# A fused four-layer kernel: first batch's steps and weight splits reordered, a smaller weight ring, more raw buffers, and extra products on TensorE

## The chip, the core and the metric

The kernel runs on one core of a Trainium2 chip. The metric is the time of one execution on the device in microseconds (us). TensorE is named PE in the profile, its weight loads PEld, VectorE is DVE, ScalarE is ACT, GpSimd is POOL, and SP is the engine that issues most of the transfers.

## The reference

The input x has 16 batches of 256 positions and 256 channels. Four layers follow each other, each added to x. Cut to what matters:

```python
# layer 0, for each batch: gates, 16 decaying scans over the positions, a small gated network, a normalisation
ctx = causal_ema(x, tau_ctx)
gated = x * sigmoid(concat(x, ctx) @ Wg.T + bg)
mod = 0.5 + sigmoid(gelu(x @ Wn1.T + bn1) @ Wn2.T + bn2)           # 16 factors for each position
traces = causal_ema(gated * mod[d], tau_raws[d])                    # d = 0..15
temporal = sum_d traces[d] * softmax(blend)[d]
x += layernorm((gelu(x @ Wsoma.T + bsoma) * sigmoid(temporal @ Wtemp.T + btemp)) @ Wout.T)
# layer 1: masked softmax pooling over the 256 positions
s = tanh(x @ W1 + b1) @ v
x += softmax(where(mask, s, NEG)) @ x / cnt
# layer 2: 8 experts and a shared one, all dense
x += sum_e coef[b, e] * ((silu(x @ Wg[e]) * (x @ Wu[e])) @ Wd[e])
# layer 3: 256 -> 1024 -> 256, a part of its second matrix chosen for each batch
x += gelu(x @ W1 + b1) @ concat(W2, We[indices[b]]) + bias
```

Layers 2 and 3 hold nearly all of the products.

## The kernel before

**Precision.** For most products each operand is split into a rounded part and a remainder (`rnd` on one engine, then `low` on another), and `mm3` (L101 to L104) makes three products of them. The first batch's layers 0 and 1 do without the split: `first_traces` and `first_pooled` make plain fp32 products.

**Layers 0 and 1** are written as generators, one per batch: `traces` (21 steps) and `pooled` (10 steps), with `first_traces` (13 steps) and `first_pooled` for batch 0. `feed` interleaves the steps of two neighbouring batches: batch 0's pooling runs beside the first steps of batch 1's traces. In `first_traces`, ph and pg are the first products, hg is a Gelu of ph, pm a product of hg, md its Tanh; from these come the 16 factors, then 16 scans of two halves each on VectorE, which TensorE adds up in PSUM (ta0). In `first_pooled` the names follow each other in a chain: t, pt, g, po, rs (a power on POOL), x1, four transposes ptr, x1T, pa, th, psc, sc (softmax), four transposes ppt, q, pp, acc, and the split x2 that the experts read. `evict(c, ...)` (L470 to L476) copies PSUM to SBUF on ScalarE for c = 0 and on VectorE for c = 1.

**Layers 2 and 3** follow a written plan of units. A chunk of an expert is 128 x 768 values (`w_e`). Batch 0 is alone for the first five experts, two chunks to a unit; batch 1 joins at the sixth ("boards"), and afterwards pairs of batches share each chunk. Each `l2_unit` makes products pg and pu, ScalarE and VectorE make h of them, ScalarE and POOL split it (hh), and the downward products (y) are issued two units later (LAG). At the end of a pair's experts come eight chunks of layer 3 (`w_f`, products q and z), with chunks chosen by batch (`w_c`).

**Weights.** `load_chunk` fetches a chunk into one of two raw buffers, rounds it on ScalarE (`w_e<-raw_e`, L89) and takes the remainder on VectorE or POOL (L96) into one of RING = 10 tiles. A chunk that has been split twice before is stored in DRAM and later reloaded whole (`w_e<-keep_e`). `prefetch` runs through the chunks in the plan's order. The small weights of layers 0 and 1 are split once (`split_small`), some before the scans' end and some beside batch 1's traces.

**Order.** The tile framework arranges the instructions of each engine by a simulated timeline, under priorities. `tc.issue_after(i)` keeps what stands under it from being arranged ahead of instruction i. `last_of` remembers such instructions. Each engine then works through its own queue in order.

Of the kernel before, what the change touches and what calls it, by code (L numbers as in the profile page):

```python
# [8 lines left out]
F32 = mybir.dt.float32  # L9
F32R = mybir.dt.float32r  # L10
I32 = mybir.dt.int32
AF = mybir.ActivationFunctionType
ALU = mybir.AluOpType
# [4 lines left out]
S = 256  # L18
# [1 line left out]
ND = 16  # L20
NE = 8
NF = 8
RING = 10
FRONT = 4
FRONT0 = 3
SLACK = 16
# [19 lines left out]
def fused_kernel(  # L46
# [24 lines left out]
    xin = ctx.enter_context(tc.tile_pool(name="xin", bufs=2))  # L71
    l0 = ctx.enter_context(tc.tile_pool(name="l0", bufs=1))
    ring = ctx.enter_context(tc.tile_pool(name="ring", bufs=RING))
    raws = ctx.enter_context(tc.tile_pool(name="raws", bufs=2))
    xs = ctx.enter_context(tc.tile_pool(name="xs", bufs=3))
    accp = ctx.enter_context(tc.tile_pool(name="accp", bufs=3))
    hp = ctx.enter_context(tc.tile_pool(name="hp", bufs=2))
# [59 lines left out]
    def split_small(c0, n, e):  # L137
        rnd("a", wh[:, c0 : c0 + n], small(c0, n))
        low(e, wl[:, c0 : c0 + n], small(c0, n), wh[:, c0 : c0 + n])
# [114 lines left out]
    def ft(tag, name, bufs=1):  # L254
        return l0.tile([P, 2, S], F32, tag=tag, name=name, bufs=bufs)
# [5 lines left out]
    def traces(b):  # L261

        xr = xin_tiles.pop(b)
        xh, xl = hl(f"x_{b}", "hA")
        rnd("a", xh, xr)
        low("g", xl, xr, xh)
        cx = ft("ta", f"ctx{b}")
        for c in range(2):
            V.tensor_tensor_scan(
                cx[:, c], decay[:, ND : ND + 1].to_broadcast([P, S]), xr[:, c], 0.0, ALU.mult, ALU.add  # L270
            )
        yield
        ch, cl = hl(f"c_{b}", "hA")
        rnd("a", ch, cx)
        low("v", cl, cx, ch)

        ph = ps_l.tile([P, 512], F32, tag="ps", name=f"ph{b}")
        for k in range(2):
            o = O_N1 + k * P
            mm3(ph[:, :S], W(0, o, P), W(1, o, P), xh[:, k], xl[:, k], k == 0, k == 1)  # L280
        hg = l0.tile([P, S], F32, tag="hg", name=f"hg{b}")
        A.activation(hg, ph[:, :S], AF.Gelu, bias=vec[:, V_BN1 : V_BN1 + 1])
        hs = l0.tile([P, S], F32R, tag="hs", name=f"hs{b}")
        rnd("a", hs, hg)
        low("v", hs[64:], hg[64:], hs[64:])
        yield
        pm = ps_l.tile([P, 512], F32, tag="ps", name=f"pm{b}")
        PE.matmul(pm[:48, :S], n2[:, 0], hs, start=True, stop=False)
        PE.matmul(pm[:48, :S], n2[:, 1], hs, start=False, stop=True)
        md = l0.tile([48, S], F32, tag="md", name=f"md{b}")  # L290
        A.activation(md, pm[:48, :S], AF.Tanh, bias=hb[:48, V_BN2 : V_BN2 + 1], scale=0.5)
        V.tensor_scalar(md, md, 0.5, 1.0, ALU.mult, ALU.add)
        mdd = dram.tile([1, ND, S], F32, tag="mdd", name=f"mdd{b}")
        nc.sync.dma_start(mdd[0], md[0:ND])
        yield
        pg = ps_l.tile([P, 2, S], F32, tag="ps", name=f"pg{b}")

        ga = ps_a.tile([P, 2, S], F32, tag="ga", name=f"gp{b}")
        for m in range(2):
            for k in range(4):  # L300
                o = O_G + k * S + m * P
                xa, xb_ = (xh[:, k], xl[:, k]) if k < 2 else (ch[:, k - 2], cl[:, k - 2])
                mm3(pg[:, m], W(0, o, P), W(1, o, P), xa, xb_, k == 0, k == 3)
        for m in range(2):
            A.activation(ga[:, m], pg[:, m], AF.Tanh, bias=hb[:, V_BG + m : V_BG + m + 1], scale=0.5)
        V.scalar_tensor_tensor(ga, ga, 1.0, xr, ALU.add, ALU.mult)
        yield
        sm = ft("sm", f"sm{b}")

        def soma():  # L310
            pso = ps_l.tile([P, 2, S], F32, tag="ps", name=f"pso{b}")
            for m in range(2):
                for k in range(2):
                    o = O_SO + k * S + m * P
                    mm3(pso[:, m], W(0, o, P), W(1, o, P), xh[:, k], xl[:, k], k == 0, k == 1)
            for m in range(2):
                A.activation(sm[:, m], pso[:, m], AF.Gelu, bias=vec[:, V_BSO + m : V_BSO + m + 1])

        tacc = ft("ta", f"ta{b}")
        for d in range(ND):  # L320
            if d % 2 == 0:
                mod = l0.tile([P, 2, S], F32, tag="mod", name=f"mod{b}_{d}", bufs=2)
                nc.sync.dma_start(mod, mdd[0, d : d + 2].partition_broadcast(P))
            bt = ft("bt", f"bt{b}_{d}", 3)
            tr = tacc if d == 0 else ft("tr", f"tr{b}_{d}", 3)
            with tc.issue_after(last_of[0].ins) if b == 1 and "h" not in last_of else nullcontext():
                for c in range(2):
                    V.scalar_tensor_tensor(
                        bt[:, c], ga[:, c], bl[:, c, d : d + 1], mod[:, d % 2], ALU.mult, ALU.mult
                    )  # L330
            for c in range(2):
                V.tensor_tensor_scan(  # L332
                    tr[:, c], decay[:, d : d + 1].to_broadcast([P, S]), bt[:, c], 0.0, ALU.mult, ALU.add
                )
            if d:
                G.tensor_tensor(tacc, tacc, tr, ALU.add)  # L336
            if b == 1 and d in rest:
                split_small(*rest[d], "g")
            if d == 5:
                soma()  # L340
            yield
        th, tl = hl(f"t_{b}", "hA")
        rnd("a", th, tacc)
        low("v", tl, tacc, th)
        xt = xt_tiles.pop(b)
        G.tensor_tensor(xt, xt, bet.unsqueeze(1).to_broadcast([P, 2, S]), ALU.add)
        held[b] = xt, sm, th, tl
        yield
# [122 lines left out]
    def evict(c, o, i):  # L471
# [3 lines left out]
        else:  # L475
            last_of["cv"] = V.tensor_copy(o, i)  # L476

    def first_traces():
        xr = xin_tiles.pop(0)
        cx = ft("ta", "ctx0")  # L480
        for c in range(2):
            last_of["cx"] = V.tensor_tensor_scan(
# [77 lines left out]
    def first_pooled():  # L560
# [19 lines left out]
        rs = l0.tile([P, 2], F32, tag="rs", name="rs0")  # L580
        for k in range(2):
            for t in range(2):
                PE.matmul(po[t], sg[:, k, t * P : (t + 1) * P], small(O_OU + k * S, S), start=k == 0, stop=k == 1)
        x1 = ft("x1", "x10")
        for t in range(2):
            V.bn_stats(st[:, t], po[t])
            V.bn_aggr(mv[:, t], st[:, t])
        V.tensor_scalar(rs, mv[:, :, 1], 4e-5, None, ALU.add)
        G.tensor_tensor(rs, rs, mhalf, ALU.pow)
        for t in range(2):  # L590
            V.scalar_tensor_tensor(po[t], po[t], mv[:, t, 0:1], gam, ALU.subtract, ALU.mult)
        yield
# [6 lines left out]
        ptr = two("ptr0")  # L599
        for c in range(2):  # L600
            for t in range(2):
                PE.transpose(ptr[c][:, t * P : (t + 1) * P], x1[:, t, c * P : (c + 1) * P], ident)
        x1T = ft("xo", "x1T0")
        for c in range(2):
            evict(c, x1T[:, c], ptr[c])
        yield
        pa = ps_l.tile([P, 512], F32, tag="ps", name="pa0")
        for k in range(2):
            PE.matmul(pa[:, :S], small(O_W1 + k * P, P), x1T[:, k], start=k == 0, stop=k == 1)
        ta = l0.tile([P, S], F32, tag="th", name="th0")  # L610
        last_of["ca"] = A.activation(ta, pa[:, :S], AF.Tanh, bias=vec[:, V_B1 : V_B1 + 1])
        yield
        psc = ps_l.tile([P, 512], F32, tag="ps", name="psc0")
        PE.matmul(psc[:, :S], vec[0:64, V_V : V_V + 1].to_broadcast([64, P]), ta[0:64], start=True, stop=True)

        sc = ft("sc", "sc0")
        mx = l0.tile([P, 2], F32, tag="mx", name="mx0")
# [9 lines left out]
        for j in range(2):  # L627
            js = slice(j, j + 1)
            V.tensor_tensor(sums[:, js], sums[:, js], cntb[:, 0, js], ALU.mult)
            V.reciprocal(sums[:, js], sums[:, js])  # L630
            last_of["cv"] = V.tensor_scalar(sc[:, j], sc[:, j], sums[:, js], None, ALU.mult)
        yield
        ppt = two("ppt0")
        for l in range(2):
            for j in range(2):
                PE.transpose(ppt[l][:, j * P : (j + 1) * P], sc[:, j, l * P : (l + 1) * P], ident)
        q = ft("bt", "q0", 3)
        for l in range(2):
            evict(l, q[:, l], ppt[l])
        yield  # L640
        pp = two("pp0")
        for l in range(2):
# [17 lines left out]
    def load_chunk(key):  # L660
# [26 lines left out]
        e = "v"  # L687
        if kind == "e" and key[1] == 0:

            e = "g" if key[2] < 2 else "v" if key[2] < 6 else "gv"[key[2] % 2]  # L690
        elif kind == "e" and key[1] < ALONE and key[2] % 3 == 0:
            e = "g"
        low(e, t[:, 1, :n], raw[:, :n], t[:, 0, :n])
# [251 lines left out]
            with tc.issue_after(last_of["cx"].ins):  # L945
                later_constants()
    with tc.issue_after(last_of["a"].ins), tc.issue_after(last_of["g"].ins), tc.issue_after(last_of["tr"].ins):
        for off, n in ((O_N1, 256), (O_G, 512), (O_G + 512, 512)):
            split_small(off, n, "g")
        prefetch(2, 0)  # L950


    n = 2
    while n_done[0] < 1:
        with tc.issue_after(last_of["ca"].ins), tc.issue_after(last_of["cv"].ins):
            next(steps)
            if n_steps[0] > FIRST + 5 and n < 6 and n_steps[0] % 2:
                prefetch(1, 0)
                n += 1
    with tc.issue_after(last_of["ca"].ins), tc.issue_after(last_of["cv"].ins):  # L960
        coefs()
        prefetch(RING - n)
# [155 lines left out]
```

## Time and profile before

| | us |
|---|---|
| median of 3 runs | 2840.18 (2839.82 to 2841.34) |
| the profiled execution, its own time | 2841.92 |
| span of that execution | 2840.2 |
| granted TensorE clock, mean | 0.994 |
| first product of an expert | 58.90 |
| TensorE busy | 2779.2 (98%) |
| VectorE, ScalarE, POOL busy | 1425.2, 1235.4, 1299.0 |

The span runs from the first to the last recorded instruction. Times inside it are counted from its start. Rows of the timeline read: start, duration, engine, source line, operation, what is written from what is read, sizes, count, and in brackets the idle time before it with what ended it. A wait row reads: who, for whom, us in total, times, longest. In a window row the pairs are the busy times of PE, PEld, DVE, ACT and POOL, each with its count of instructions, then the granted clock of TensorE, the share of the DMA engines and GB/s.

### The profile page before, as it was taken

What the parts mean: (1) busy time and instruction counts of PE and PEld (TensorE: products, weight loads), DVE (VectorE), ACT (ScalarE), POOL (GpSimd) and SP (SyncE); (2) the same over time, 40 slices, a digit from 0 to 9 for tenths busy, and PEclk for the clock granted to TensorE, in tenths of its full rate; (3) what the DMA queues carried; (4) which work ended last, traced back from release to release, by engine and by line L of the source; (5) the groups of instructions that cost most, each with busy time, mean ns of one, the idle gap of its engine ahead of it and who ended that gap; (6) DMA issues with size and microseconds to landing.
All of it is one profiled execution on the core that took longest, in us unless ns stands there. A gap on an engine that the chain in (4) does not pass through costs nothing. (4 is left out here: it accounts for less than half of the span.)

```text
span 2840.2 us, 36878 instructions
## 1 busy us (share of the span) xinstructions
PE 2779.2 (98%) x13604; PEld 2335.0 (82%) x13604; DVE 1425.2 (50%) x2646; ACT 1235.4 (43%) x2043; POOL 1299.0 (46%) x986
## 2 busy tenths in 40 slices
PE   7889989999999999999999999999999999999998
PEld 4877779888888888888888888888888888888887
DVE  7888766665665364544545445453444542222222
ACT  5555544546444533435334443334433453323433
POOL 5764654544544353544534445444444443333333
PEclk9999999999999999999999999999999999999999
DMA  4444645546443533324433153331523242222552
GB/s 125 136 148 122 196 162 181 185 131 230 148 164 117 180 115 104 119 77 135 150 110 106 40 180 112 111 117 58 177 101 112 91 169 90 89 89 76 192 198 83
DMA packets 114693, 371.23 MB, mean 131 GB/s; under 512 B 12642, under 2 KB 30930, under 8 KB 114514
## 3 DMA queue, kind: packets, MB, share of 16 engines
q1 hardware_dynamic: 114082, 368.82, 39.2%
q8 instruction: 108, 1.77, 0.3%
q14 instruction: 71, 0.58, 0.1%
q10 hardware_dynamic: 432, 0.06, 0.0%
HBM read 304.62 MB, written 64.21 MB: 130 GB/s over the span
## 5 line engine op out<-in xcount | busy, mean ns | idle before, releaser
L96 POOL TENSOR_TENSOR hh<-h,hh 128x512 fp32r<-128x512 f32 x640 | 848.7, 1326 | 1317.4 <-ACT hh L89 1297.4
L745 DVE TENSOR_TENSOR h<-h,pu 128x512 f32<-128x512 f32 x576 | 393.5, 683 | 941.9 <-PE pu L104 813.0
L89 ACT ACTIVATE hh<-h 128x512 fp32r<-128x512 f32 x640 | 403.4, 631 | 936.0 <-DVE h L745 914.9
L744 ACT ACTIVATE h<-pg 128x512 f32<-128x512 f32 x576 | 342.8, 595 | 317.7 <-PE pg L104 236.5
L102 PE MATMUL pg<-x,w_e 128*128 128x512 f32 (+1 forms) x1232 | 466.3, 379 | 10.1 <-ACT h L744 3.9
L102 PE MATMUL pu<-x,w_e 128*128 128x512 f32 (+1 forms) x1232 | 464.9, 377 | 7.5 <-ACT h L744 7.4
L104 PE MATMUL pg<-x,w_e 128*128 128x512 f32 (+1 forms) x1232 | 465.3, 378 | 1.8 <-DVE w_e L96 1.4
L103 PE MATMUL y<-hh,w_e 128*128 128x512 f32 (+1 forms) x1232 | 463.7, 377 | 2.5 <-POOL hh L96 2.5
L103 PE MATMUL pg<-x,w_e 128*128 128x512 f32 (+1 forms) x1232 | 464.7, 377 | 0.8 <-POOL x L96 0.8
L103 PE MATMUL pu<-x,w_e 128*128 128x512 f32 (+1 forms) x1232 | 463.7, 376 | 0.0
L104 PE MATMUL pu<-x,w_e 128*128 128x512 f32 (+1 forms) x1232 | 463.7, 376 | 0.0
L104 PE MATMUL y<-hh,w_e 128*128 128x512 f32 (+1 forms) x1232 | 463.1, 376 | 0.0
L102 PE MATMUL y<-hh,w_e 128*128 128x512 f32 (+1 forms) x1232 | 415.2, 377 | 2.9 <-ACT hh L89 1.6
L336 POOL TENSOR_TENSOR ta<-ta,tr 128x512 f32<-128x512 f32 x225 | 308.9, 1373 | 84.4 <-DVE tr L332 72.1
L332 DVE TENSOR_TENSOR_SCAN tr<-decay,bt 128x256 f32<-128x256 f32 x450 | 284.7, 669 | 0.0
L102 PEld LDWEIGHTS pg<-x,w_e 128*128 128x128 f32 x1232 | 232.5, 189 | 53.1 <-ACT h L744 4.8
L102 PEld LDWEIGHTS pu<-x,w_e 128*128 128x128 f32 x1232 | 232.6, 189 | 51.2 <-ACT h L744 9.9
L103 PEld LDWEIGHTS y<-hh,w_e 128*128 128x128 f32 x1232 | 232.8, 189 | 46.3 <-POOL hh L96 4.6
L104 PEld LDWEIGHTS pg<-x,w_e 128*128 128x128 f32 x1232 | 232.7, 189 | 44.9 <-DVE w_e L96 2.4
L102 PEld LDWEIGHTS y<-hh,w_e 128*128 128x128 f32 x1232 | 231.5, 189 | 45.7 <-ACT hh L89 2.6
L104 PEld LDWEIGHTS y<-hh,w_e 128*128 128x128 f32 x1232 | 232.7, 189 | 41.8
L104 PEld LDWEIGHTS pu<-x,w_e 128*128 128x128 f32 x1232 | 232.5, 189 | 41.9
(279 smaller groups left out, 3220.8 us busy)
## 6 DMA issues: line engine op xcount, KB each, us to landing
w_e<-keep_e SPq DMA_DIRECT2D x216, 768.0 KB, 4.4
raw_e<-in_wexp_dram SPq DMA_DIRECT2D x144, 384.0 KB, 4.3
keep_e<-w_e SPq DMA_DIRECT2D x72, 768.0 KB, 4.3
mod<-mdd SPq DMA_DIRECT2D x120, 256.0 KB, 3.7
w_f<-keep_f SPq DMA_DIRECT2D x56, 384.0 KB, 3.5
raw_c<-in_comb_dram SPq DMA_DIRECT2D x32, 260.0 KB, 2.8
xr<-in_xT_dram SPq DMA_DIRECT2D x16, 256.0 KB, 3.7
xt<-in_x_dram SPq DMA_DIRECT2D x16, 256.0 KB, 2.7
```

Source lines behind the costliest of these rows:

```text
L89: last_of["ca"] = A.activation(out_, in_, AF.Copy)
L96: i = (V if e == "v" else G).tensor_tensor(out_, in_, h.bitcast(F32), ALU.subtract)
L102: PE.matmul(o, wh, xh, start=start, stop=False, **kw)
L103: PE.matmul(o, wh, xl, start=False, stop=False, **kw)
L104: last_of["pe"] = PE.matmul(o, wl, xh, start=False, stop=stop, **kw)
L332: V.tensor_tensor_scan(tr[:, c], decay[:, d : d + 1].to_broadcast([P, S]), bt[:, c], 0.0, ALU.mult, ALU.add)
L336: G.tensor_tensor(tacc, tacc, tr, ALU.add)
L744: A.activation(h, ps_g, AF.Silu)
L745: last_of["h"] = V.tensor_tensor(h, h, ps_u, ALU.mult)
```

## The change

Buffers: the ring has 9 tiles instead of 10, and there are 4 raw buffers instead of 2; the two together take as much memory as before. Extra products: `warm(n)` issues n products of the identity with itself into a PSUM tile that nobody reads, nine ahead of the first product and five, one, two, eight and one in `first_pooled`, each group behind the product named. Order: the first splits of small weights take turns with the first two chunks; chunks 2 and 3 are fetched behind rs, chunk 4 behind th, chunk 5 behind sc; chunks 2 and 3 have their remainder on POOL, chunk 0 on VectorE; both halves of x1T and of q are evicted on ScalarE; the splits beside batch 1's traces are not arranged ahead of batch 0's x2.

```diff
-RING = 10
+RING = 9
-    raws = ctx.enter_context(tc.tile_pool(name="raws", bufs=2))
+    raws = ctx.enter_context(tc.tile_pool(name="raws", bufs=4))
...
             if b == 1 and d in rest:
-                split_small(*rest[d], "g")
+                with tc.issue_after(last_of[0].ins):
+                    split_small(*rest[d], "g")
...
+    idle = ps_y.tile([P, 512], F32, tag="y1", name="idle")
+
+    def warm(n, after=None):
+
+        with tc.issue_after(after.ins) if after is not None else nullcontext():
+            for _ in range(n):
+                PE.matmul(idle[:, :P], ident, ident, start=True, stop=True)
+
     def first_traces():
         xr = xin_tiles.pop(0)
+        warm(9)
...
-                PE.matmul(po[t], sg[:, k, t * P : (t + 1) * P], small(O_OU + k * S, S), start=k == 0, stop=k == 1)
+                w = small(O_OU + k * S, S)
+                i = PE.matmul(po[t], sg[:, k, t * P : (t + 1) * P], w, start=k == 0, stop=k == 1)
+        warm(5, i)
...
-        G.tensor_tensor(rs, rs, mhalf, ALU.pow)
+        last_of["rs"] = G.tensor_tensor(rs, rs, mhalf, ALU.pow)
...
+        warm(1, i)          # behind the transposes ptr
         x1T = ft("xo", "x1T0")
         for c in range(2):
-            evict(c, x1T[:, c], ptr[c])
+            evict(0, x1T[:, c], ptr[c])
...
+        warm(2, i)          # behind pa
...
-        last_of["ca"] = A.activation(ta, pa[:, :S], AF.Tanh, bias=vec[:, V_B1 : V_B1 + 1])
+        last_of["ca"] = last_of["th"] = A.activation(ta, pa[:, :S], AF.Tanh, bias=vec[:, V_B1 : V_B1 + 1])
...
+        warm(8, i)          # behind psc
...
-            last_of["cv"] = V.tensor_scalar(sc[:, j], sc[:, j], sums[:, js], None, ALU.mult)
+            last_of["cv"] = last_of["sc"] = V.tensor_scalar(sc[:, j], sc[:, j], sums[:, js], None, ALU.mult)
...
+        warm(1, i)          # behind the transposes ppt
         q = ft("bt", "q0", 3)
         for l in range(2):
-            evict(l, q[:, l], ppt[l])
+            evict(0, q[:, l], ppt[l])
...
-            e = "g" if key[2] < 2 else "v" if key[2] < 6 else "gv"[key[2] % 2]
+            e = "vgggvv"[key[2]] if key[2] < 6 else "gv"[key[2] % 2]
...
-        for off, n in ((O_N1, 256), (O_G, 512), (O_G + 512, 512)):
+        prefetch(1, 0)
+        split_small(O_N1, 256, "g")
+        prefetch(1, 0)
+        for off, n in ((O_G, 512), (O_G + 512, 512)):
             split_small(off, n, "g")
-        prefetch(2, 0)
...
             next(steps)
-            if n_steps[0] > FIRST + 5 and n < 6 and n_steps[0] % 2:
+        if n == 2 and "rs" in last_of:
+            with tc.issue_after(last_of["rs"].ins), tc.issue_after(last_of["ca"].ins):
+                prefetch(2, 0)
+            n += 2
+        if n == 4 and "th" in last_of:
+            with tc.issue_after(last_of["th"].ins):
                 prefetch(1, 0)
-                n += 1
+            n += 1
+        if n == 5 and "sc" in last_of:
+            with tc.issue_after(last_of["sc"].ins), tc.issue_after(last_of["ca"].ins):
+                prefetch(1, 0)
+            n += 1
```

## The prediction

> **What bounds the kernel now.** I read the page first, then the windows by stage, then the waits of the stage that loses most, then the timeline of the stretch that the diff edits.
>
> ```profile
> span 2840.2 us, 36878 instructions
> ...
> PE 2779.2 (98%) x13604; PEld 2335.0 (82%) x13604; DVE 1425.2 (50%) x2646; ACT 1235.4 (43%) x2043; POOL 1299.0 (46%) x986
> ```
>
> TensorE is the bound over the whole. What can be won is where it waits, or where its clock is low:
>
> ```profile
> 59.00:116.00 57.00, 51.96 (x398) 49.83 (x399) 52.42 (x94) 29.44 (x43) 42.38 (x28) 0.97 0.44 140
> 116.00:187.00 71.00, 59.15 (x450) 55.92 (x449) 50.96 (x81) 45.54 (x74) 40.26 (x27) 0.98 0.48 148
> 187.00:420.00 233.00, 214.86 (x1065) 179.23 (x1066) 186.10 (x329) 123.51 (x200) 131.20 (x92) 0.96 0.49 154
> 420.00:2800.00 2380.00, 2376.42 (x11412) 2001.13 (x11412) 1083.94 (x2027) 986.44 (x1631) 1036.52 (x796) 1.00 0.39 129
> ```
>
> Columns: window, length, busy PE, PEld, DVE, ACT, POOL, granted clock. From 420 to 2800 TensorE idles 3.6 us: nothing is to be had there, only lost. Batch 0 (to 58.9 us), its experts alone (59 to 187) and the first pair (to 420) are where the change can act. In 116 to 187, 450 products, nearly all of 256 columns and 0.119 us from start to start, need 53.5 of 71 us. Who holds them:
>
> ```profile
> ACT w_e L89 <- DMA raw_e<-in_wexp_dram: 15.4, 15, 2.8
> ...
> PE pg L102 <- ACT w_e L89: 3.1, 2, 2.1
> PE pu L102 <- ACT h L744: 2.3, 2, 1.4
> PE pso L102 <- DVE acc L461: 2.0, 1, 2.0
> PE y L102 <- ACT hh L89: 1.6, 2, 0.9
> ```
>
> ScalarE works in order: it stands before a rounding whose raw chunk has not landed, and the h behind it is late for TensorE. One such case, rows of ACT and then of PE:
>
> ```profile
> 164.37 0.85 ACT L89 ACTIVATE w_e<-raw_e 128x768 fp32r<-128x768 f32 x1 [2.81 <-DMA raw_e<-in_wexp_dram]
> 165.23 1.28 ACT L744 ACT_TABLE_LOAD   x1
> 166.53 0.60 ACT L744 ACTIVATE h<-pg 128x512 f32<-128x512 f32 x1
> ...
> 167.18 0.39 PE L102 MATMUL pu<-x,w_e 128*128 128x256 f32 x1 [1.41 <-ACT h L744]
> ```
>
> The raw chunk is late since only two raw buffers exist: a transfer takes 3.2 us to land and can't be issued before the split of two chunks earlier. From 65.96 to 197.19 us ScalarE rounds 39 chunks, one every 3.45 us.
>
> The front, TensorE's timeline and two windows:
>
> ```profile
> 45.52 0.33 PE L602 MATMUL ptr0g<-ident,x 128*128 128x128 f32 x1 [0.47 <-DVE x L594]
> ...
> 47.40 2.11 PE L609 MATMUL pa<-x1T,small_a 128*128 128x256 f32 x4 [1.04 <-ACT x1T L474]
> 50.07 1.22 PE L614 MATMUL psc<-th,vec 64*128 64x256 f32 x2 [0.56 <-ACT th L611]
> ...
> 55.03 1.22 PE L644 MATMUL pp0g<-q,x 128*128 128x256 f32 x2 [0.45 <-ACT q L474]
> ...
> 58.90 0.38 PE L102 MATMUL pg<-x,w_e 128*128 128x256 f32 x1 [0.53 <-ACT x L89]
> ```
> ```profile
> 46.00:48.00 2.00, 0.95 (x4) 0.51 (x4) 1.94 (x4) 1.34 (x3) 0.00 (x0) 0.88 0.53 136
> 48.00:50.00 2.00, 1.51 (x4) 0.50 (x2) 1.19 (x2) 0.46 (x1) 1.29 (x1) 0.50 0.59 192
> ...
> 56.00:58.00 2.00, 2.00 (x7) 1.55 (x5) 0.12 (x2) 0.00 (x0) 0.00 (x0) 0.56 0.84 324
> ```
>
> The clock is halved from about 47.5 to 57.8 us, under pa, psc, the transposes and pp: an x4 of pa takes 2.11 us, while the four instructions of pt at full clock (37.98 to 38.95) take 0.97.
>
> **The change, part by part.** Orders below are those of the two built programs.
>
> *Nine products at the start.* Each is two instructions of 128 columns; half of a cold 256-column one (0.51 us from start to start) is 0.26, so 18 take 4.6 us from 1.4 us, when ident is written, to 6.0; the first real product waits for its DMA to 5.93. Cost 0 to +1 (if the weight loads of 0.34 us bound them), and ph and pg then run at full clock: 4 us become 2. That gain is not kept. In the new order ScalarE rounds two weight tiles before it loads the Gelu table for hg. Their transfers land at 4.96 + 3.0 = 7.96 and 5.33 + 3.3 = 8.63 us, so hg starts at 8.63 + 0.62 + 1.28 = 10.5 instead of 8.02, and pm, reached at 10.69 before, starts at 11.0. VectorE's md ends at 13.1 in the trace since it sits through POOL's split (10.46 to 12.97), and would so again. Bounds 0 to +0.5; I take +0.2.
>
> *Scans (16.5 to 36.3).* VectorE is solid with 32 scans; nothing changes. w_e_0_0's low half (0.95 us) moves to VectorE behind them, into its idle 1.63 us before the copy of t: 0.
>
> *POOL.* One split of 1.8 us fewer stands ahead of x_1 and of rs. In the trace rs' TENSOR_SCALAR on VectorE takes 0.61 us instead of 0.16, up to the end of POOL's x_1 split: -0.45, x starts at 44.5 instead of 44.98.
>
> *Evictions and their queue.* Both x1T halves go to ScalarE (0.36 each) right behind the transposes: done by 46.7; before, the halves started at 46.98 and 47.81. pa at full clock is done at 47.3. But c_1, hg1 and hs1 (0.61 + 0.45 + 0.42) now stand between x1T and th on ScalarE, so th starts at 48.2 (49.54 before). w_e_0_4's rounding (0.83) and its low half (0.95) stand ahead of the scores on VectorE: 50.5 (51.33 before), Exp at 51.0 (51.80). w_e_0_5 and md follow, then both q halves: done 54.2 (55.9 before). The second eviction on ScalarE costs 0.36 and spares VectorE's queue more.
>
> *Products between (5, 1, 2, 8, 1).* 34 instructions of 0.12 us, about 4 us, in gaps of 1 to 2 us; full clock keeps the eight of pp at 0.215 instead of 0.42: end 56.0 instead of 58.4. First expert product at 56.5 instead of 58.9: -2.4, with +0.2 above -2.2. Should the eight behind psc run cold, they end 1.2 us after the softmax is ready; that is in the range.
> Here a rule speaks against the change. The Trainium skill, "TensorE: Matmul & The Clock Gate", section "Part 1: The HAM clock gate", has the clock fall after at least one idle window of about 3.4 us. No gap of TensorE between 38 and 47.5 us exceeds 1.52 us, and the clock fell: the 3.4 us to 47.5 held some 1.8 us of work. By the rule the products have nothing to keep; pa would end at 48.6, the second half of q at 54.6, pp last until 57.9, and the front would give -0.7; by the rows it gives -2.2. I take the rows.
>
> *Raw buffers 2 to 4.* The transfer of a chunk can start four splits ahead; ScalarE's 15.4 us (116 to 187) and 17.7 us (59 to 116) before raw chunks go. Of TensorE's waits in 116 to 187, 7.9 us stand behind ScalarE (3.1 + 2.3 + 1.6, and 0.9 of psc). What is late next is batch 1's own chain (2.0 + 0.8 us of waits) and ring releases. I take -6, bounds -10 and 0, and -1 for the clock windows behind those gaps. In 59 to 116 VectorE is busy 52.4 of 57 us with batch 1's scans and takes over as the bound: -1, bounds -3 and +2.
>
> *Ring 10 to 9.* Same bytes. Between the last product that reads a ring buffer's old chunk and the first that reads the new one, the order holds 6.4 us or more of products in the single-batch stage before, and 3.3 to 5.4 us for the tight chunks after. Refilling now is rounding (0.84) and low half (0.95 on VectorE, 1.85 on POOL), 1.8 to 2.7 us, plus queueing behind scans (0.6 to 2.4). It mostly fits: +2, bounds 0 and +12. In the last chunks of each pair (w_f, reloaded whole) the room falls from 5.2 to 3.9 us in the last stage, against 3.4 to 4.1 us to land: eight stages at 0 to 0.4, I take +1. Elsewhere the room is 8 us or more: 0.
>
> *Waits for last_of on batch 1's splits, and 187 to 420.* They move work that VectorE and ScalarE have room for; unknown order effects, 0, bounds -4 and +4.
>
> Sum: -2.2 - 7 - 1 + 2 + 1 = -7.2. The profiled execution has a span of 2840.2 and took 2841.92, 1.7 above the median of 2840.18; on the median the forecast is 2833.0.
>
> **The rivals.** *Hidden anyway*: VectorE and batch 1's chain take the place of the raw waits at once, TensorE waits at the boarding of batch 1 (pso, 2.0 us) instead, and the front alone is kept: 2840.2 - 2.2 - 1 = 2837. For: VectorE at 92% in 59 to 116. Against: 72% in 116 to 187.
> *The ring becomes the bound, slower*: the rounding waits for TensorE's release and the low half queues behind scans. If each of the 20 units of batch 0 alone loses 0.8 us net of what the raw buffers give, that is +16, less 2.2, with +2 in the w_f stages: 2856; it is slower than before from 0.2 us a unit. For: room of 3.3 us against up to 5.1 needed in the worst queue. Against: median room 6.5.
> *The change doesn't do what it says*: not so; the order has the 26 products where the diff puts them.
>
> **How the numbers follow.** About 0.2% (5.7 us) is what a measurement of this kernel can tell from no change. Forecast with its own spread, 2824 to 2834.5: 0.57. Hidden, 2834.5 to 2846: 0.27. Ring, 2846 to 2860: 0.16. The range 2823 to 2845 leaves out about 0.2, most of it the ring.
>
> **What would show it.** Right: granted clock 1.00 from 40 to 60 us and first expert product at 56 to 57; raw waits of ACT under 5 us in 59 to 187; boarding of batch 1 (187 now) at about 177. Wrong: ACT w_e waiting on PE y for over 10 us there, or the boarding no earlier than the front's gain; TensorE gaps before w_f products late in the trace.

## The result, and the profile after

| us | before | after |
|---|---|---|
| median, eight runs each, same chip | 2841.65 (2839.82 to 2843.0) | 2851.52 (2847.43 to 2852.08) |
| ratio, 95% interval | | 1.0033 [1.0023, 1.0042] |
| profiled execution: span, own time | 2840.2, 2841.92 | 2850.0, 2851.94 |
| first product of an expert | 58.90 | 63.51 |
| batch 1's pooling is added (acc, L461/L462) | 181.5 | 194.1 |

The change is slower by 0.33%, some 9.4 us by that ratio and 9.9 between the medians; faster by 7.2 had been forecast. The page of the changed kernel, its first lines:

```profile
span 2850.0 us, 36990 instructions
...
PE 2786.0 (98%) x13656; PEld 2343.4 (82%) x13656; DVE 1451.3 (51%) x2643; ACT 1240.5 (44%) x2050; POOL 1299.8 (46%) x987
```

Nothing in totals gives it away. The windows by stage, as before (length, busy PE, PEld, DVE, ACT, POOL, granted clock):

```profile
59.00:116.00 57.00, 52.68 (x406) 50.91 (x407) 52.76 (x95) 33.35 (x53) 41.98 (x26) 0.97 0.53 165
116.00:187.00 71.00, 55.18 (x428) 53.01 (x427) 56.38 (x76) 42.41 (x71) 41.45 (x26) 0.92 0.56 170
187.00:420.00 233.00, 208.27 (x1032) 172.37 (x1031) 185.56 (x323) 115.70 (x189) 120.08 (x88) 0.96 0.39 123
420.00:2800.00 2380.00, 2379.16 (x11432) 2004.54 (x11431) 1100.92 (x2042) 996.96 (x1642) 1042.44 (x798) 1.00 0.39 131
```

The loss is where the change acts: from 116 to 420 the records show 55 products fewer in the same time, in part at a lower clock; past 420 TensorE idles less than before (0.8 us of 2380, 3.6 before). Two places carry it. The first is in the front, on VectorE and POOL. In the kernel before, POOL had no gap there and VectorE's queue went straight to the second half of t:

```profile
36.23 3.16 POOL L96 TENSOR_TENSOR wl<-small_a,wh 128x256 fp32r<-128x256 f32 x3
39.35 3.57 POOL L96 TENSOR_TENSOR w_e<-raw_e,w_e 128x768 fp32r<-128x768 f32 x2
42.88 1.26 POOL L96 TENSOR_TENSOR x<-xr,x 128x512 fp32r<-128x512 f32 x1
...
37.96 0.42 DVE L476 COPY t<-ta 128x256 f32<-128x256 f32 x1 [1.63 <-ACT t L474]
```

The changed kernel, the same two engines and TensorE:

```profile
37.07 0.71 POOL L96 TENSOR_TENSOR wl<-small_a,wh 128x256 fp32r<-128x256 f32 x1
37.10 5.71 DVE L96 TENSOR_TENSOR w_e<-raw_e,w_e 128x768 fp32r<-128x768 f32 x1
...
37.76 1.80 POOL L96 TENSOR_TENSOR w_e<-raw_e,w_e 128x768 fp32r<-128x768 f32 x1
39.52 2.47 POOL L96 TENSOR_TENSOR wl<-small_a,wh 128x512 fp32r<-128x512 f32 x2
42.73 0.41 DVE L477 COPY t<-ta 128x256 f32<-128x256 f32 x1
...
43.20 1.22 PE L579 MATMUL pt0g<-t,small_b 128*128 128x256 f32 x2 [3.23 <-DVE t L477]
```

Chunk 0's low half, 0.95 us elsewhere, stood on VectorE for 5.71. POOL started 0.03 us earlier and had four instructions back to back, to 41.99; VectorE's ended 0.82 later. The second half of t, next in VectorE's queue, came at 42.73 instead of 37.96, TensorE waited 3.23 us, and its granted clock was half from 42.97 to 49.79.

Behind that the 17 products ran at full clock in this execution, and the real ones with them, on TensorE's timeline:

```profile
54.09 1.13 PE L622 MATMUL pa<-x1T,small_a 128*128 128x256 f32 x4 [1.30 <-ACT hg L282]
...
56.41 2.05 PE L485 MATMUL idle<-ident 128*128 128x128 f32 x16
...
60.98 0.70 PE L660 MATMUL pp0g<-q,x 128*128 128x256 f32 x2 [0.20 <-ACT q L475]
...
63.51 0.38 PE L102 MATMUL pg<-x,w_e 128*128 128x256 f32 x1 [0.53 <-ACT x L89]
```

pa takes 1.13 us instead of 2.11. Before it stands a wait of 1.30 us for hg, which the section on e7 and e15 comes back to. The second place is the boarding of batch 1. The waits of 116 to 187 (who, for whom, us, times, longest):

```profile
ACT hh L89 <- DVE h L761: 17.1, 9, 3.7
...
PE ppt L446 <- DVE sc L438: 7.3, 1, 7.3
...
PE pg L102 <- DVE q L96: 1.9, 1, 1.9
```

ScalarE's 15.4 us for raw chunks are down to 1.6, as forecast; it now stands 17.1 us for VectorE's h (3.4 before). And TensorE stands 7.3 us at once for batch 1's softmax: batch 0's experts have run ahead (the fifth expert's y is added at 174.5, 194.8 before, though the first started 4.6 us later), and batch 1's chain comes later than before (its product psc at 171.9, 155.0 before).

### The profile page after: what moved, and what is told of

The parts are those of the page before. It is cut to its first block, busy times and chain, and to the rows that moved or that the text cites. A ratio compares the mean times of both kernels' runs of the same rounds, so it can differ in the third digit from the quotient of the medians.

```text
span 2850.0 us, 36990 instructions
## 1 busy us (share of the span) xinstructions
PE 2786.0 (98%) x13656; PEld 2343.4 (82%) x13656; DVE 1451.3 (51%) x2643; ACT 1240.5 (44%) x2050; POOL 1299.8 (46%) x987
## 4 chain that ended last, share of the span: by engine, by line
PE 89%; DVE 6%; issue 2%; ACT 1%; DMA 1%; POOL 0%; DVEq 0%; ACTq 0%; POOLq 0%
PE pg L102 9%; PE pg L103 9%; PE pg L104 9%; PE pu L102 9%; PE pu L103 9%; PE pu L104 9%; PE y L102 8%; PE y L104 8%; PE y L103 8%; DVE tr L332 1%; DVE w_e L96 1%; PE q L102 1%; PE q L103 1%; DVE bt L328 1%; PE q L104 1%
## 5 line engine op out<-in xcount | busy, mean ns | idle before, releaser
L102 PEld LDWEIGHTS pg<-x,w_e 128*128 128x128 f32 x1232 | 232.5, 189 | 56.5 <-DVE h L761 15.8
```

What stands on the lines that cost most here:

```text
L102: PE.matmul(o, wh, xh, start=start, stop=False, **kw)
```

## The experiments

Theory A: the front's loss is that one VectorE instruction. Theory B: the boarding's loss is the order that the new buffers bring. Theory C: the nine products at the start cost. The rivals: the ring's size by itself, the products as such, the queue orders of the front. "Built order" below is the order of each engine's queue in the program, as the framework arranged it. All were timed in five rounds beside the kernel before; differences are to that. The four columns of lateness come from one profiled execution each, against the trace of before (58.90, 181.5, 428.6, 2840.2; the third is an expert's y of the second pair's boarding). A single execution can lie up to 6.2 us from its median (e1, e3), a profiled one lay up to 3.8 off (e15), so medians decide and the columns say where. The first column moves by itself: five kernels with the front of the kernel before or only the nine products added (before, e3, e9, e12, e14) have it at 57.95 to 59.04, as the clock is half for 6.8 to 13.7 us in that stretch.

| run | median | difference | ratio, 95% | first expert product | batch 1's pooling | 428.6 | span |
|---|---|---|---|---|---|---|---|
| the change | 2851.52 | +9.9 | 1.0033 [1.0023, 1.0042] | +4.6 | +12.6 | +12.6 | +9.8 |
| e1_low_on_pool | 2842.54 | +1.4 | 1.0006 [1.0000, 1.0013] | +1.7 | +9.5 | +2.9 | +0.6 |
| e2_no_products | 2853.25 | +12.1 | 1.0041 [1.0027, 1.0055] | +8.6 | +14.5 | +13.3 | +9.8 |
| e3_buffers_alone | 2844.63 | +3.5 | 1.0015 [1.0008, 1.0021] | 0.0 | +6.7 | +5.1 | +2.4 |
| e4_old_buffers | 2848.38 | +7.2 | 1.0029 [1.0017, 1.0041] | +5.0 | +5.4 | +7.2 | +5.0 |
| e5_pool_old_buffers | 2842.81 | +1.2 | 1.0006 [0.9998, 1.0014] | +1.8 | +4.1 | +6.4 | +3.7 |
| e6_pool_no_nine | 2844.91 | +3.3 | 1.0011 [1.0005, 1.0018] | +1.6 | +7.9 | +6.1 | +3.2 |
| e7_pool_no_nine_old | 2843.23 | +1.6 | 1.0005 [0.9997, 1.0013] | +0.9 | +3.3 | +3.7 | +0.9 |
| e8_products_evictions | 2842.33 | +0.7 | 1.0004 [0.9995, 1.0012] | -1.4 | +1.2 | +2.7 | +2.0 |
| e9_buffers_held | 2841.33 | -0.2 | 1.0000 [0.9992, 1.0009] | -1.0 | +0.7 | +0.3 | -3.0 |
| e10_change_held | 2846.90 | +5.3 | 1.0020 [1.0013, 1.0027] | +3.8 | +5.4 | +6.2 | +5.3 |
| e11_best | 2839.28 | -2.3 | 0.9990 [0.9982, 0.9998] | -3.1 | 0.0 | +0.2 | -2.7 |
| e12_ring_alone | 2849.64 | +8.1 | 1.0025 [1.0016, 1.0034] | -0.1 | -2.0 | +6.6 | +7.5 |
| e13_low_alone | 2848.02 | +6.4 | 1.0021 [1.0012, 1.0029] | +6.3 | +6.5 | +7.5 | +6.3 |
| e14_nine_alone | 2843.91 | +2.3 | 1.0010 [1.0001, 1.0018] | +0.1 | +1.8 | +2.3 | +1.8 |
| e15_change_mended | 2842.56 | +0.9 | 1.0003 [0.9995, 1.0012] | +1.1 | +4.5 | +5.3 | +4.4 |
| e16_best_held_longer | 2840.53 | -1.1 | 0.9997 [0.9989, 1.0005] | -3.0 | -1.2 | +0.8 | -2.8 |

**One instruction on VectorE: e1 and e13.** e1 is the changed kernel with chunk 0's low half back on POOL:

```diff
-            e = "vgggvv"[key[2]] if key[2] < 6 else "gv"[key[2] % 2]
+            e = "ggggvv"[key[2]] if key[2] < 6 else "gv"[key[2] % 2]
```

> Changed kernel with one letter different: chunk 0's low half back on POOL. Theory A (the front's loss is that one VectorE instruction, held up through POOL's run of four): the instruction and the 3.23 us wait of pt0g for t go, t's second half is copied at about 38 instead of 42.7 us, first expert product at 59 to 60 instead of 63.5, and since the stage behind is bound by the order of products and batch 1's chain, 3 to 5 us come back at the end: 2847 to 2848.5. Rival (the loss is in the products on TensorE and the queue order): first expert product stays at 62 to 64, 2851.

Measured: first expert product 60.55, 3.0 us earlier than in the change and 0.6 over theory A's band; but 9 us came back at the end, not 3 to 5. At the boarding e1 is still 9.5 us late; 6.6 of them are made good by 428.6. Part of that is a second thing. e1's built order differs from the changed kernel's at the second boarding too: the first product of the tenth expert unit is TensorE's 1603rd as in the kernel before, not its 1615th (extra products not counted). Where it is the 1615th (the change, e2, e3, e6), the stretch that lies from 319.3 to 354.1 us in the trace of before, from one y to another, takes 42 to 43 us; where it is the 1603rd, 35 to 39. No run changed that alone. So e13 has only the instruction, in the kernel before:

```diff
-            e = "g" if key[2] < 2 else "v" if key[2] < 6 else "gv"[key[2] % 2]
+            e = "g" if key[2] == 1 else "v" if key[2] < 6 else "gv"[key[2] % 2]
```

> Kernel before with chunk 0's low half on VectorE instead of POOL, nothing else; TensorE's order is unchanged. Theory A: it becomes ready while POOL runs its splits back to back and is held until that run has a gap; VectorE is stuck for 4 to 7 us before the second half of t, first expert product 3 to 5 us later (62 to 64), and since the order behind is unchanged the lateness is carried to the end: 2844 to 2847. Rival (it fits into VectorE's idle 1.63 us as the prediction had it, and what cost in the changed kernel was the order of POOL's queue): first expert product at 58.5 to 59, 2840.5 to 2842.

Its timelines of VectorE, POOL and TensorE:

```profile
36.32 5.71 DVE L96 TENSOR_TENSOR w_e<-raw_e,w_e 128x768 fp32r<-128x768 f32 x1
...
36.27 3.17 POOL L96 TENSOR_TENSOR wl<-small_a,wh 128x256 fp32r<-128x256 f32 x3
39.40 1.80 POOL L96 TENSOR_TENSOR w_e<-raw_e,w_e 128x768 fp32r<-128x768 f32 x1
...
42.41 1.22 PE L569 MATMUL pt0g<-t,small_b 128*128 128x256 f32 x2 [3.23 <-DVE t L476]
```

The same 5.71 us, again until POOL's run of four is over (41.20) and 0.83 more; the same 3.23 us of TensorE, and the clock halved from 41.93 to 48.76 and from 52.17 to 65.82. First expert product 65.22 and end 2848.02, both later even than expected, and the 6.3 us are carried unchanged to the end: 1.0021 [1.0012, 1.0029]. One instruction of 0.95 us on the wrong engine costs 6.4 us, the slow clock behind it included. Theory A's cost is shown, by taking the instruction out (e1) and by putting it in alone (e13). That it is POOL's run that holds it is read from the ends in the traces; no run moved POOL's run away.

**The buffers: e3, e12, e4.** e3 is the kernel before with both sizes changed, e12 with the ring alone:

```diff
-RING = 10
+RING = 9
-    raws = ctx.enter_context(tc.tile_pool(name="raws", bufs=2))
+    raws = ctx.enter_context(tc.tile_pool(name="raws", bufs=4))    # e3 only
```

> Kernel before with RING 9 and four raw buffers, nothing else. Theory B (the buffers alone change the order of TensorE's products in the single-batch stage: only 12 products are left between batch 1's psc and its ppt where 46 stood before, and TensorE waits there): front unchanged, first expert product at 58.9, batch 1's pooling 6 to 9 us later than before, at 187 to 190, end 2846 to 2850. Rival (the ring or the raw buffers are harmless, the loss is the front's that is carried along): boarding no later than 183, 2838 to 2842.

> Kernel before with RING 9, two raw buffers kept. The prediction's step (+2 in the single-batch stage, +1 in the w_f stages, bounds 0 and +12) gives 2843 to 2845, with ScalarE waiting for the ring's release some us more in 59 to 187. Rival (the ring costs nothing, the order that it brings has batch 1's chain earlier: 21 low halves ahead of the scores instead of 23): 2839 to 2842. Rival (the ring is the bound): over 2847.

e3: pooling at 188.2, as theory B said, end a little under its band. e12: the ring alone costs 8.1 us, over the band of the prediction's step and in that of the rival that the ring is the bound. Batch 1's pooling is not late there (-2.0); the lateness grows behind it, in 187 to 420. ScalarE's waits in that window, the kernel before:

```profile
ACT w_e L89 <- DMA raw_e<-in_wexp_dram: 17.9, 18, 3.7
...
ACT w_e L89 <- PE y L104: 7.0, 3, 3.5
```

and e12:

```profile
ACT w_e L89 <- DMA raw_e<-in_wexp_dram: 26.8, 21, 2.8
ACT w_e L89 <- PE y L104: 12.0, 6, 3.5
```

With one tile fewer the rounding stands 12.0 us instead of 7.0 before a tile that TensorE's y still reads, and 26.8 instead of 17.9 for raw chunks. That a raw buffer emptied late makes the next transfer late fits, but is not shown to be the cost: none of TensorE's products there is listed as waiting for a chunk, and what grew is their wait for VectorE's h, from 1.2 to 6.0 us. The built order differs too (36 products between batch 1's psc and ppt, 46 before). So the ring's 8.1 us are measured and their cause stays open. Two more raw buffers on top of that (e3 against e12) give 5.0 us back. So the trade "one ring tile for two raw buffers" is a loss of 8.1 and a gain of 5.0. e4 is the changed kernel with the old sizes (RING 10, two raw buffers):

> Changed kernel with RING 10 and two raw buffers as before; front, products and waits stay. Theory B: the order of the products behind the front is that of the kernel before again, so of the 9.8 us only the front's part stays: 2844 to 2847. Rival (the loss is the front's, or batch 1's waits for last_of): 2850 to 2852.

Measured +7.2: the front's 5.0 us, constant to the boarding, with 2 more by 428.6. The lateness does not grow at batch 1's boarding, where with the new sizes it grew by 8; that half of theory B holds. The end, 2848.38, lies over the band: only some 3 us came back, not the 4.5 to 7.5 expected.

**What the buffers do to the order: e9, e10.** In the built order of e3 and of the change alike, batch 1's scores stand behind 47 roundings of chunks on ScalarE and 29 or 30 low halves on VectorE; in the kernel before behind 35 and 22 (the text of e9 has 23, a miscount). In the framework's simulated timeline the chunks land earlier, and their splits stand ahead of the chain. TensorE has 12 products left between psc and ppt, where it had 46, to bridge a softmax. e9 is e3 with those splits placed behind batch 1's latest step; e10 is the whole change with the same lines:

```diff
+        held_by = [last_of["b1"].ins] if kind == "e" and "b1" in last_of and n_done[0] < 2 else []
+        with tc.issue_after(held_by[0]) if held_by else nullcontext():
-        rnd("a", t[:, 0, :n], raw[:, :n])
+            rnd("a", t[:, 0, :n], raw[:, :n])
...
+            if b == 1:
+                last_of["b1"] = i      # behind each scan of traces, and behind t, s, u, ths, sc and q
```

(low is wrapped in the same way.)

> Kernel before with RING 9 and four raw buffers, and with the splits of the chunks that are loaded in the single-batch stage placed behind batch 1's latest step in the queues. In the built order batch 1's scores then stand behind 24 low halves on VectorE and 39 roundings on ScalarE, where the buffers alone have 30 and 47 and the kernel before 23 and 35; TensorE has 30 products between psc and ppt instead of 12. Theory B (the buffers' loss is this order: chunk splits that are ready earlier are queued ahead of batch 1's chain, and the boarding waits for the chain): batch 1's pooling at 180 to 184 instead of 188.2, end 2838 to 2841 against 2844.6 for the buffers alone. Rival (VectorE is simply full, or ring 9 holds the chunks back): pooling at 187 or later, 2843 to 2846.

> Changed kernel, whole, with the same splits placed behind batch 1's steps. Theory B: of the 12.6 us by which batch 1's pooling came late some 6 to 8 go, pooling at 186 to 188; the front's 4.6 us stay: 2844 to 2847. Rival (order is not it): pooling at 192 to 195, 2850 to 2852.

TensorE's waits from 116 to 195, in e3:

```profile
PE ppt L445 <- DVE sc L437: 6.7, 1, 6.7
PE pso L102 <- DVE acc L461: 2.7, 1, 2.7
PE pg L102 <- DVE q L96: 1.9, 1, 1.9
```

and in e9:

```profile
PE ptr L406 <- ACT hg L282: 2.6, 1, 2.6
PE pg L102 <- DVE q L96: 2.3, 1, 2.3
PE pu L102 <- ACT h L761: 1.8, 1, 1.8
...
PE pso L102 <- DVE acc L475: 0.9, 1, 0.9
```

The wait at ppt is gone, batch 1's pooling comes at 182.2 instead of 188.2 (1.0 of these 6.0 us is the front's, where the clock fell later in this execution), and the buffers' 3.5 us are gone with it (1.0000 [0.9992, 1.0009]). In the changed kernel it comes at 186.9 instead of 194.1, and the end falls by 4.6 us. Both are in the bands of theory B, but for 0.3 us at the end of e9: the boarding's loss is an order, not a shortage of an engine.

**Both repairs: e15.** The change with chunk 0's low half on POOL and the splits placed:

> Changed kernel with two repairs: chunk 0's low half on POOL, and the splits of the single-batch stage behind batch 1's latest step. If these two are the whole loss, it should not be slower than the kernel before: first expert product at 59.5 to 60.5, pooling of batch 1 at 181 to 185, 2839 to 2842. Rival (ring 9 or the front's order costs besides): 2843 to 2846.

1.0003 [0.9995, 1.0012]: not told from the kernel before, with an interval that does not touch the change's. What the two causes leave is 0.9 us, between -1.4 and +3.4. Its profiled execution took 2846.33, the longest of its runs, so its last three columns are of little use. What stays open is how they share: undone one at a time, they give back 9.0 us (e1) and 4.6 (e10) of 9.9, so they overlap.

**Low half and buffers together, and the nine products: e5, e6, e7, e14.** e5 is e4 with chunk 0's low half on POOL; e6 is e1 without `warm(9)`; e7 is e5 without it; e14 is the kernel before with it.

> Changed kernel with chunk 0's low half on POOL and with RING 10 and two raw buffers; products and orders of the front stay. If the two losses found so far (the instruction on VectorE, the order that the buffers bring) are all there is but the 1.7 us by which the first expert product still came late with the low half on POOL (60.55 against 58.90), the shift is constant behind the front: first expert product at 60.5, end 1.5 to 2.5 us over the kernel before, 2842 to 2843.5. Rival (something else in the change costs too): 2844 to 2846. Rival (the front's lateness is absorbed later): 2840 to 2841.5.

> Changed kernel with chunk 0's low half on POOL and without the nine products at the start. Theory C (the nine are a loss: they bring ph and pg forward, TensorE then stands 2.4 us before hg, the clock falls at 12.8 under ctx's products, pb and pso, and t comes 2.5 us later): clock at 1.00 from 10 to 47, t's products at 38 instead of 40.5, first expert product at 57.5 to 58.5. Behind it the order that the buffers bring still costs some 4 us at the boarding: end 2839.5 to 2842. Rival (the late hg, by the two roundings ahead of it, is the cause, not the products): t at 40, first expert product at 60, 2842 to 2843.5.

> Changed kernel with chunk 0's low half on POOL, without the nine products, with RING 10 and two raw buffers: of the change only the reordered front and the 17 products are left. Theories A, B and C together: first expert product at 57.5 to 58.5, a shift of -0.5 to -1.5 us that stays constant: 2838.5 to 2840.5. Rival (the late hg costs, or a front that ends earlier meets ring chunks that come no earlier): 2841 to 2843.

> Kernel before with the nine products at the start, nothing else. Theory C (they bring ph and pg forward and leave TensorE a lull before hg and md, so that the clock falls once between 12 and 20 us and pso, pb and with them the scans come later): t's products 0.5 to 2.7 us later than 37.98, first expert product at 59.5 to 61.5, 2841.5 to 2844. Rival (no cost, as the prediction had it, 0 to +0.5): t at 37.5 to 38.3, 2841 to 2842.

e5 landed in its band, e6 and e7 ended over both of theirs. Of theory C little is left. In e5 and e1 the clock did fall at 12.7 to 12.8 us and t came at 40.5; without the nine e7 had t at 37.85, but e6 at 39.60 with the clock halved at 16.05 all the same: VectorE's constants had stood behind POOL's splits (md started at 12.95), and TensorE was idle for 1.7 us. And e15, with the nine and the same front as e1, had full clock from 6.35 to 47.31 and t at 38.16: whether the clock falls there differs between executions of one front. In e14 t came at 38.09 and the first expert product at 59.04, no later than before. The late hg itself is there in each kernel with the nine; in e14:

```profile
11.14 0.63 PE L506 MATMUL pm<-hg,vec 64*48 64x256 f32 x2 [1.98 <-ACT hg L494]
```

The end of e14 is 2.3 us over the kernel before, just past its interval; its lateness is 0.4 us up to 111 us and 1.9 by 134. There TensorE waits 2.0 us for w_e (1.0 before) and 0.9 for POOL's hh (none before); what made these late was not found. Removing the nine (e6 against e1, e7 against e5) gained nothing at the end.

**What the reordered front is worth: e7, e15.** In these two t comes on time (its products at 37.85 and 38.16, 37.98 before), so that they show the rest of the front as the change orders it. The first expert product is at 59.76 and 60.01, some 1 us later than before, where the prediction had 2.4 us earlier. Rows of TensorE and VectorE in e15:

```profile
48.06 2.08 PE L636 MATMUL pa<-x1T,small_a 128*128 128x256 f32 x4 [1.30 <-ACT hg L282]
...
52.07 3.78 PE L499 MATMUL idle<-ident 128*128 128x128 f32 x16
...
53.77 0.35 DVE L660 TENSOR_SCALAR sc<-sc,sums 128x256 f32<-128x256 f32 x1
...
56.08 0.41 PE L665 MATMUL ppt0g<-ident,sc 128*128 128x128 f32 x1
```

x1T is complete at 47.13, but pa waits until hg, at 48.01, has read ph: both lie in the only PSUM buffer that the pool `ps_l` has (bufs=1). ScalarE has hg behind both evictions now, and ahead of them before. Over that gap of 1.30 us the clock falls, to half from 47.31 to 57.55, with the products in place. The eight behind psc then take 3.78 us and end at 55.85, 1.7 us after the first half of the softmax is ready; the transposes ppt stand behind them. It is the same in e7, and in e6, where ppt starts 5.15 us after psc (3.17 before).

**The 17 products and the evictions: e2, e8.** e2 is the change without the 17 (the nine stay); e8 is the kernel before with the 17 and with all four evictions on ScalarE.

> Changed kernel without the 17 products behind po, ptr, pa, psc and ppt (the nine at the start stay). Theory A: they keep pa and pp at full clock as the trace shows (pa 1.13 instead of 2.11, eight instructions of pp 1.7 us shorter), so without them the first expert product comes 2 to 3 us later, at 65.5 to 66.5, and the end 1 to 3 us later: 2853 to 2854.5. Rival (the products stand in the way, and idle time there is worth more): first expert product at 61 to 63 and 2849 to 2850.

> Kernel before with the 17 products behind po, ptr, pa, psc and ppt and with all four evictions of x1T and q on ScalarE; prefetches, splits and buffers as before. The prediction's step for these parts: clock 1.00 from 40 to 60, pa 1.1 instead of 2.1 us, the eight of pp 1.7 us shorter, first expert product at 56.5 to 57.5, and the shift stays: 2838 to 2839. Rival (the softmax chain on VectorE and ScalarE sets the time and the products only fill it, ending behind it): first expert product at 57.5 to 58.5, 2839.5 to 2840.5. Rival (chunks of the first expert are late for an earlier front): end as before.

In e2 the first expert product is at 67.5, 4.0 us later than in the change, and the end at 2853.25: they help that front (the two ends' intervals overlap). In e8 it is at 57.52, with the clock half from 47.29 to 50.70 in spite of the products, and the end is where it was (1.0004 [0.9995, 1.0012]). Products and evictions were not timed apart. The lead of 1.4 us was lost within 10 us, on the raw buffers: ScalarE finished its two chunks early and then stood 3.37 us for the next (1.81 in the kernel before), at 67.10. The last rival fits best.

**The best version: e11, e16.** e11 is e8 with RING 9, four raw buffers and the splits placed as in e9; e16 places them behind the steps of batches 1 to 3.

> Kernel before with the 17 products, the four evictions on ScalarE, RING 9, four raw buffers, and the splits placed behind batch 1's steps. If the front's gain of 1.4 us was lost to a raw chunk that came late (the wait of 3.37 us at 67 in the products-and-evictions run), four raw buffers keep it, and the placed splits let TensorE board earlier: first expert product at 57.5, pooling of batch 1 at 178 to 182, 2835 to 2838.5. Rival (batch 1's chain sets the boarding whatever the front does): 2839 to 2842.

> The best version so far (2839.3), with the splits behind the steps of batches 1 to 3 instead of batch 1 alone. In the best version the lead of 4.2 us at 319 was given back by 429 (+0.2), where the second pair boards; in the built order TensorE now has 52 products between batch 2's psc and ppt instead of 30. Theory B applied there: the lead at 429 is 2 to 4 us, end 2835 to 2838. Rival (the lead is lost to VectorE's load, not to the order): 2838.5 to 2841.

e11, TensorE's timeline, and its window of 59 to 116:

```profile
47.04 1.13 PE L632 MATMUL pa<-x1T,small_a 128*128 128x256 f32 x4 [0.49 <-ACT x1T L488]
...
54.63 0.59 PE L670 MATMUL pp0u<-q,x 128*128 128x256 f32 x2
55.76 0.38 PE L102 MATMUL pg<-x,w_e 128*128 128x256 f32 x1 [0.53 <-ACT x L89]
```
```profile
59.00:116.00 57.00, 49.88 (x385) 48.86 (x385) 54.86 (x92) 29.30 (x44) 47.01 (x30) 0.94 0.54 167
```

First expert product at 55.76, clock at 1.00 from 10.19 to 88.69: 3.1 us ahead of the kernel before. Batch 1's pooling comes no earlier than before (0.0): VectorE is busy 54.86 of 57 us in the window shown, with batch 1's scans. It still ends at 0.999 [0.9982, 0.9998], 2.3 us faster than the kernel before, in the band of its rival. e16's hold of the later batches shortened the second boarding but cost some 2.5 us ahead of it (the sixth expert's y at 236.9, 234.4 in e11) and gained nothing over e11; its end lies in the band of its rival, VectorE's load, which no run tested by itself.

## Why the prediction was wrong, step by step

Two groups of terms can be set against runs. For the buffers alone the sum has -5 (-6, -1, -1, +2 and +1); e3 measured +3.5. For the front it has -2.2; the changed front on the old buffers measured +7.2 (e4), and +1.2 with the low half back on POOL (e5).

- **Nine products at the start** (taken +0.2): hg at 10.6 and pm at 11.1 came as worked out, and t no later in e14. A term of at most +2.3 us at the end remains, with its place (111 to 134 us) but no mechanism.
- **Scans: 0 for the moved low half. This step failed.** It fitted the instruction's 0.95 us into VectorE's idle 1.63 and asked only what VectorE does there, not what POOL does. POOL's run was in the trace of before (36.23 to 44.14 without a gap), and the next paragraph of the same text counted the 0.45 us that rs lost to the end of that run. Low halves of this very shape that took 2.0 to 2.1 us beside POOL were in that trace too (at 60.78 and 87.41). Measured alone: 5.71 us for the instruction, +6.4 at the end. The term had no bounds, and no rival held it.
- **POOL, rs** (-0.45): rs took 0.16 in the changed kernel as forecast; it could not matter behind a loss of 4.6.
- **Evictions and their queue; products between** (-2.4 with rs). **This failed too.** The step put hg behind the evictions and did not ask what pa waits for besides x1T: it waits for hg, 0.93 us beyond x1T in e15. With t on time the front came to 59.8 and 60.0 (e7, e15), 56.5 was forecast. The case that the step left in its range, eight products running cold behind psc, is what happened there. The 55.76 of e11 is near the forecast by another way, with ScalarE's old order. In the changed kernel itself t was late: from its second half to the first expert product it takes 20.8 us, 20.9 before, since pt and po ran at half clock.
- **The clock.** The Trainium skill's rule of one idle window of about 3.4 us ("TensorE: Matmul & The Clock Gate", "Part 1: The HAM clock gate") would have had the products keep nothing. In the traces the clock fell in or within 0.7 us after far shorter gaps: before pa these were 1.05 us in the kernel before, 0.92 in e8, and 1.30 in e1, e5, e6, e7 and e15. With 0.49 it stayed (e11, e16). But in the changed kernel, e4 and e10 it stayed over 1.30 as well, 3 to 4 us after a slow stretch. So the rows were the better guide than the rule, and the forecast of full clock from 40 to 60 us came true only in e11 and e16; what decides is not shown.
- **That the front's gain lasts. This failed too.** In e8 earliness was lost within 10 us (raw chunks). In e11 batch 1's pooling came no earlier, and a lead of 4.2 us at 315 was gone by 428.6. Lateness of the front was carried whole in e13 and e4; that of the boarding was in part made up (e3, 6.7 us at the pooling, 2.4 at the end). The sum took every gain as kept.
- **Raw buffers 2 to 4** (-7 and -1): the waits went as said, and 5.0 us came with them at ring 9. **Its price for what comes next failed:** the step named batch 1's chain and priced it with the waits of the old order (2.8 us). The new order is built on the earlier chunks; there TensorE waits 7.3 us at ppt, 2.8 at pso (2.0 before) and 1.9 at q. Held back, the same splits cost nothing (e9).
- **Ring 10 to 9** (+2 and +1): measured +8.1, inside the bounds of 0 and +12. **The place failed:** the single-batch stage lost nothing by its pooling (-2.0), the stages past 428.6 at most 0.9; the loss is in the pair stage of 187 to 420, for which the step had said "8 us or more: 0". Why it is lost there stays open.
- **Waits for last_of**: no run took them out alone. With the other two causes mended, nothing that can be measured is left for them (e15).
- **The rivals.** *Hidden anyway* named the mechanism of the boarding, VectorE and batch 1's chain, and stopped at no gain. *The ring becomes the bound* had the sign, but placed the loss in the units of batch 0 alone. By its own sum it is slower than before from 0.01 us a unit, not 0.2 (20 units, +2, -2.2).
- **The signs.** The raw waits of ScalarE fell under 5 us in 59 to 187, as a right forecast would have it (1.6), without the gain. The other two signs went against it: the clock was half from 42.97 to 49.79, and batch 1 boarded later, not earlier (pooling at 194.1, 181.5 before).

## What to carry to other kernels

Before moving an element-wise instruction to an idle VectorE, look at what POOL does at that moment: here a run of POOL instructions without a gap held it for 5.71 us, and all that was queued behind it. When a buffer grows, compare the built orders first: work that becomes ready earlier is queued earlier, ahead of the chain that the next stage waits for, and holding it back can win back what the buffer cost. When an eviction moves ahead in a queue, look for what else its reader waits for. A lead at the front of a pipeline is lost at the first resource that was just in time.

## What was not expected of the hardware

- The low half on VectorE was not let in between POOL's instructions. The Trainium skill ("SBUF — State Buffer", section "SBUF: two separate sides") says that a VectorE instruction with two SBUF inputs and a GpSimd instruction that reads SBUF exclude each other, and that whichever starts first holds the shared ports for the whole instruction. Freed at the end of POOL's first, it would have run from 37.78 and been done by 38.7, an estimate from its 0.95 us elsewhere. It was done at 42.81, after the fourth, and in e13 at 42.03, after the fourth again.
- That is the exception. In the trace of before 39 other low halves of this shape on VectorE are stretched, each by one POOL instruction only. In 14 of them POOL's next one follows without a gap, and it is then POOL that is held:

```profile
87.41 2.00 DVE L96 TENSOR_TENSOR w_e<-raw_e,w_e 128x768 fp32r<-128x768 f32 x1
...
87.31 1.28 POOL L96 TENSOR_TENSOR hh<-h,hh 128x512 fp32r<-128x512 f32 x1
88.56 2.00 POOL L336 TENSOR_TENSOR ta<-ta,tr 128x512 f32<-128x512 f32 x1
```

The ta before these two took 1.29. A hold through four was seen only at this place, in the five kernels that have chunk 0's low half on VectorE (the change, e2, e4, e10, e13). Why there is not shown.
- Not every VectorE instruction is held. In e6 POOL made 13 products bt in 16.01 us without a pause from 20.64 us on, and VectorE 26 scans in 16.01 us from 21.94 on, 0.62 us each, so that both were busy throughout from 21.94 to 36.65.
- The clock was half from 42.97 us on in the changed kernel and from 41.93 in e13, each time across 3.23 us of idle TensorE; in e11 it stayed at 1.00 for 78.5 us where, from 37 to 56, the 17 products leave no gap over 0.6 us.
